# Four graph layers on one core: row sums folded by DMA to the heads' own partitions, gates transposed on VectorE, layer 3 in four column tiles, and tiling changes counted in the plan

## The chip, the cores and the metric

The kernel runs on one core of a Trainium2 chip. A core has TensorE (PE, the matrix engine), VectorE (DVE), ScalarE (ACT), GpSimd (POOL), SyncE (SP, which only issues transfers) and 16 DMA engines. DMAs are issued here from SP's and POOL's queues; those that add to what stands at their destination are issued from POOL. The time is device microseconds of one execution. The median of several runs counts.

## What is computed

32 graphs of 512 nodes with 256 features go through four layers. All share one adjacency matrix. Each layer's output is added to its input and normalised. Cut to what matters:

```python
# x: (32, 512, 256), adj: (512, 512)
def layer0(x):                    # 8 heads of 32
    q, k, v = split(x @ w_qkv)
    attn = softmax(where(adj > 0, q @ k.T / sqrt(32), -1e9))
    x = layernorm(x + attn @ v)
    return layernorm(x + relu(x @ w1 + b1) @ w2 + b2)
def layer1(x):                    # one head, scores s1[n] + s2[m]
    h = x @ W
    return softmax(mask(leaky_relu(s1[:, None] + s2[None, :]))) @ h
def layer2(x):                    # scores (x W1)(x W2)^T
    return relu(softmax(mask(leaky_relu((x @ W1) @ (x @ W2).T))) @ (x @ W3))
def layer3(x):                    # 4 heads of 64, scores as in layer 1
    return elu(softmax(mask(leaky_relu(e_src + e_dst))) @ q)
for layer in (layer0, layer1, layer2, layer3):
    x = layernorm(x + layer(x))
```

## The kernel before

Everything stays in SBUF in float32. A graph's nodes lie in four chunks of 128 partitions (NC = 4), its features in two (KC = 2). Probabilities are kept transposed: a buffer `p` of 128 x 4 x 512 (1 MiB) holds, for 128 source nodes m on the partitions, four stretches of 512 target nodes n. They aren't normalised before they meet the values; the output is divided by the row sums afterwards. In layers 1 and 2 the values carry a column of ones, so that the sums come out of the same matmul. In layers 0 and 3 the outputs are computed transposed (head features on the partitions, nodes along the free axis), and the sums over m are made apart.

PE works in four tilings: full 128 x 128 matmuls; row tiles of 32 x 128 for the scores of layer 0 (`exps`, L1034, four heads side by side); column tiles of 128 x 32 for the outputs of layer 0 (L1093, four heads) and for the sums (L1065, L1281); column tiles of 128 x 64 for the outputs of layer 3 (L1306, two heads). In the plan these are `tiling=0`, 1, 2 and 3.

The row sums of layer 0: for each half of the heads (g) there are four buffers p (m = 0 to 3). `collect` adds them by accumulating DMAs (`add_dma`, issued at L972 on POOL): p1 to p0, p3 to p2, p2 to p0. What is left are two totals, `low` and `high`, with 128 partial sums per head and node. A fold adds the upper 64 partitions of `low` to its lower 64, another the lower 64 of `high` to its upper 64, a copy on SP's queue (L1112) brings these to the upper 64 of `low`, and four matmuls with a constant `pick` (L1065) sum over the partitions. ACT copies the sums out of PSUM (`sums_back`), four transposes (L985) bring nodes onto partitions, and DVE takes reciprocals (L994). Layer 3 has two pairs of buffers; after one add and one fold inside each buffer, four matmuls (L1281) sum. The last graph (`at_once`) sums all buffers on PE instead.

`gates` (layers 1 and 3) needs a row of gate values on all partitions: exponentials into `gs`, one transpose on PE (L1182), a copy by ACT (L1184), a store to DRAM on SP (L1186) and a load that spreads the row over all partitions (L1192, into G). DVE then makes p from G (L1211, L1290).

The order of the work on every engine is made when the program is built. Each piece is recorded as an `Op` with its engine, a cost in ns, its buffers and its tiling. `Plan.place` simulates the engines by these costs: at each step it takes the piece that can start first, and among those the one with the earliest due time. Up to six graphs (WAYS) are under way at once. Due times come from a pace per graph (PACE) and a curve of eleven points, with own curves for the first four and last five graphs. A DMA is two pieces, its issue on POOL or SP and the transfer on one modelled DMA server. The costs only choose the order. On the chip, each engine takes its instructions in that order and waits for its inputs. In `place` before, a change of tiling puts 100 ns (SWITCH) ahead of the piece.

Of the kernel before, what the change touches and what calls it, by code (L numbers as in the profile page):

```python
# [30 lines left out]
PACE = 81.87  # L31
STAY = 0.00
START = (0, 10.17, 59.24, 97.18, 85.64)
EARLY = 186.52

TENTHS = (0, 35.72, 65.32, 68.92, 152.58, 202.32, 246.27, 266.73, 356.34, 362.66, 490.49)
FIRST = (
    (0, 35.72, 65.32, 62.35, 138.44, 202.98, 246.27, 266.73, 356.34, 362.66, 490.49),
    (-28.44, 35.72, 73.98, 55.02, 197, 202.32, 246.27, 266.73, 356.34, 362.66, 490.49),
    (-31.13, 30.72, 65.32, 68.92, 152.58, 202.32, 246.27, 266.73, 356.34, 362.66, 490.49),  # L40
    (0, 35.77, 65.37, 68.97, 152.63, 202.32, 246.27, 266.73, 356.34, 362.66, 490.49),)
LAST = (
    (0, 35.72, 65.32, 68.92, 152.58, 202.32, 246.27, 266.73, 354.73, 363.36, 490.49),
    (0, 35.72, 65.32, 68.92, 152.58, 202.32, 246.27, 266.73, 356.34, 362.66, 490.49),
    (0, 35.72, 65.32, 68.92, 152.58, 202.26, 246.21, 266.73, 356.34, 412.91, 557.81),
    (-0.21, 35.51, 65.11, 68.71, 152.37, 202.11, 226.96, 232.14, 316.44, 341.17, 500.04),
    (-6.23, 29.49, 59.09, 8.93, 61.49, 76.67, 155.18, 191.54, 257.43, 316.36, 394.47),)
# [391 lines left out]
SIGNAL = 70  # L439
SWITCH = 100  # L440
# [11 lines left out]
class Op:  # L452
    def __init__(self, engine, ns, run, graph, rank, port, lag, tiling):
        self.engine, self.ns, self.run, self.graph, self.rank = engine, ns, run, graph, rank
        self.port, self.lag, self.tiling = port, lag, tiling
        self.then, self.missing, self.slots, self.ready = [], 0, [], 0.0


class Plan:
# [19 lines left out]
    def __call__(self, engine, ns, run, reads=(), writes=(), port=False, lag=0, tiling=0):  # L479
        op = Op(engine, ns, run, self.graph, self.rank, port, lag, tiling)  # L480
# [41 lines left out]
    def place(self, urgency, ways, stay=0.0, early=1e12, run=True):  # L522
# [13 lines left out]
        port, port_by, end, tiling = 0.0, None, 0.0, 0  # L536
        self.trace = []
# [21 lines left out]
        while todo:  # L559
            choice = None  # L560
            for e, ops in waiting.items():
                found = []
                for op in ops:
# [8 lines left out]
                    if choice and t > choice[0]:  # L572
                        continue
                    wants = {}
                    for s in op.slots:
                        if s.index is None:
                            wants.setdefault(s.kind, []).append(s)
                    if all(safe(op, kind, new) for kind, new in wants.items()):
                        for kind, new in wants.items():
                            t = max(t, sorted(free[kind])[len(new) - 1][0])  # L580
                        if op.tiling != tiling and e is PE:
                            due += stay
                        found.append((t, due, op))
                if found:
                    best = min(found, key=lambda f: f[:2])
                    if choice is None or best[0] < choice[0]:
                        choice = best
            assert choice, "no instruction can be placed: too few buffers"
            t, _, op = choice
            if op.engine is PE and op.tiling != tiling:  # L590
                t, tiling = max(t, engines[PE] + SWITCH), op.tiling
            waiting[op.engine].remove(op)
# [6 lines left out]
            engines[op.engine] = t + op.ns  # L599
            if op.port:  # L600
                port, port_by = t + op.ns, op.engine
            done = t + op.ns + op.lag + SIGNAL
# [7 lines left out]
            for other in op.then:  # L610
                other.missing -= 1
                other.ready = max(other.ready, done if other.engine != op.engine or op.lag
                                  else t + op.ns)
# [6 lines left out]
            ended[op.graph] = max(ended.get(op.graph, 0.0), t + op.ns + SIGNAL)  # L620
# [9 lines left out]
def fast_path(  # L630
# [50 lines left out]
        "e1": (6, [P, NC * H3]), "gs": (2, [P, NC * H3]), "ri": (3, [P, NC * H0]),  # L681
        "gT": (2, [NC * H3, P]),
# [27 lines left out]
    nc.vector.memset(far, 0.0)  # L710

# [36 lines left out]
    def prepare():  # L748
# [30 lines left out]
        for c in range(NC):  # L779
            dve(690, lambda c=c: nc.vector.tensor_scalar(  # L780
                T(edges)[:, c, :], T(raws[c // 2])[:, c % 2, :].bitcast(I32), 0.0, None, ALU.is_gt),
                [(raws[c // 2], c)], [(edges, c)])
        for m in range(NC):
# [6 lines left out]
            plan(PE, 440, run, [edges], [bank])  # L790
            dve(690, lambda bank=bank, m=m: nc.vector.tensor_copy(T(edge_t)[:, m, :], T(bank)),
                [bank], [(edge_t, m)])
            dve(400, lambda m=m: nc.vector.tensor_scalar(
# [23 lines left out]
        for c in range(NC):  # L817
            off = Slot("e")
            dve(690, lambda c=c, off=off: nc.vector.tensor_tensor(
                T(off), T(edges)[:, c, :], T(raws[c // 2])[:, c % 2, :].bitcast(I32), ALU.not_equal),  # L820
                [edges, (raws[c // 2], c)], [off])
            dve(690, lambda c=c, off=off: nc.vector.tensor_reduce(
# [65 lines left out]
    def evac(dst, to, src, frm, n, writes):  # L888

        act(170 + n * 0.84, lambda: nc.scalar.activation(to(T(dst)), frm(T(src)), AF.Copy),  # L890
            [src], writes)

    def transposed(src, width=0):

        dst = Slot("t")
        for c0 in range(0, NC, 2):
# [7 lines left out]
            plan(PE, 440, run, [(src, c0), (src, c0 + 1)], [bank])  # L904
# [4 lines left out]
    def project_t(w, col, xT, dst, k):  # L909
# [7 lines left out]
        plan(PE, 1720, run, [w, xT], [bank])  # L917
        evac(dst, lambda t: t[:, k, :], bank, lambda b: b, N, [(dst, k)])

    def project(xT, w, col, width, dst):  # L920

        per = N // width
        for c0 in range(0, NC, per):
# [9 lines left out]
            plan(PE, per * KC * width * 1.69, run, [w, xT], [bank])  # L933
# [4 lines left out]
    def normalise(y, dst):  # L938

        st, mv, rs, nm = Slot("st"), Slot("mv"), Slot("rs"), Slot("rs")  # L940
        for c in range(NC):
# [3 lines left out]
            dve(600, run, [(y, c)], [(st, c), (mv, c)])  # L945
# [3 lines left out]
        act(420, deviations, [mv], [rs])  # L949
        dve(300, lambda: nc.vector.scalar_tensor_tensor(  # L950
# [102 lines left out]
    def layer0(xs, at_once):  # L1053
# [27 lines left out]
        for g in range(KC):  # L1081
            av, ps = Slot("bank"), []
            for m in range(NC):
# [14 lines left out]
                if m % 2:  # L1098
                    collect(g, m, ps)
# [337 lines left out]
```

## Time and profile before

| | |
|---|---|
| Median of 3 runs | 2895.84 us (2895.43 to 2897.85) |
| Span of the profiled execution | 2891.7 us |
| PE busy | 2832.4 us, 98% |
| DVE busy | 2443.2 us, 84% |
| ACT busy | 1885.5 us, 65% |
| POOL busy | 865.9 us, 30% |
| DMA engines, mean from 500 to 2500 us | 73% |
| PE busy, 0 to 100, 100 to 200 and 2800 to 2892 us | 83.3, 91.8 and 66.4 us |
| Mean granted TensorE clock | 0.993 |

Busy time is the time in which at least one instruction of the engine was running. Matmuls overlap each other, so their mean duration is longer than their distance from start to start. In the views, a fp32 matmul stands as two records, one for each pass; a transpose as one. "128*32" is the tile of PE. In a view of waits, "A <- B: 9.7, 6, 2.7" says that A waited for B 9.7 us in total, 6 times, 2.7 us at longest. In a timeline the columns are the start in us, the length in us, engine, line, operation, tiles, shapes, and "x8" for eight records merged.

### The profile page before, as it was taken

Reading aid. Unit: us, or ns where it says so; the run is one execution under the profiler, and the core shown is the slowest. Engines: PE = TensorE matmul, PEld = TensorE weight load, DVE = VectorE, ACT = ScalarE, POOL = GpSimd, SP = SyncE. Lnnn points to the kernel's source line nnn. Section 1 sums busy time; section 2 is a strip of 40 time slices with the busy share of each in tenths; the row PEclk is TensorE's granted clock in tenths of the full one; section 3 lists DMA queues with packets and bytes.
Section 4 is the critical chain, followed back from the end, with each engine's and each line's share of the span. In section 5 each row is a group of like instructions: output and inputs, shape, how many; then the busy total and the mean of one; then the engine's idle time right before and its main releaser. Section 6 shows DMA issues by size and latency. Waiting matters only on the chain.

```text
span 2891.7 us, 39629 instructions
## 1 busy us (share of the span) xinstructions
PE 2832.4 (98%) x14014; PEld 1579.2 (55%) x14014; DVE 2443.2 (84%) x4076; ACT 1885.5 (65%) x4104; POOL 865.9 (30%) x962
## 2 busy tenths in 40 slices
PE   8899999999999999999999999999999999999996
PEld 3355555555555555555555555555555555554562
DVE  5568888888888988888988888988888888888877
ACT  4566667666667666666666666666676666676553
POOL 1233333232333232332232333232333323333312
PEclk9999999999999999999999999999999999999998
DMA  6856777777777777777777777776776777775125
GB/s 168 169 110 142 150 159 164 154 144 160 145 161 153 159 149 158 149 160 157 147 152 150 157 157 155 152 160 144 162 157 150 155 153 146 161 163 115 35 55 132
DMA packets 101149, 424.44 MB, mean 147 GB/s; under 512 B 10256, under 2 KB 46224, under 8 KB 59152
## 3 DMA queue, kind: packets, MB, share of 16 engines
q0 software_dynamic: 49600, 325.08, 57.2%
q1 hardware_dynamic: 51344, 96.75, 11.6%
q8 instruction: 113, 1.85, 0.2%
q14 instruction: 92, 0.75, 0.1%
HBM read 63.38 MB, written 17.10 MB: 28 GB/s over the span
## 4 chain that ended last, share of the span: by engine, by line
PE 92%; DVE 3%; DMA 2%; issue 1%; ACT 1%; POOL 0%; SPq 0%; ACTq 0%; DVEq 0%; POOLq 0%
PE bank L929 15%; PE bank L915 11%; PE bank L1034 9%; PE bank L1093 8%; PE bank L1306 8%; PE bank L1221 7%; PE bank L1244 7%; PE bank L1260 7%; PE bank L902 5%; PE bank L1136 4%; PE bank L1148 4%; PE bank L1017 2%; DMA p<-p 1%; PE bank L1281 1%; PE bank L1065 1%
## 5 line engine op out<-in xcount | busy, mean ns | idle before, releaser
L972 POOL DMA_DIRECT2D p<-p x372 | 322.3, 871 | 1787.8 <-DMA p<-p 568.4
L1086 DVE TENSOR_TENSOR p<-p,edge_t 128x2048 f32<-128x2048 f32 x256 | 618.2, 2424 | 59.7 <-ACT p L1038 59.5
L890 ACT ACTIVATE t<-bank 128x512 f32<-128x512 f32 x640 | 373.5, 596 | 384.2 <-PE bank L915 125.4
L1038 ACT ACTIVATE p<-bank 128x512 f32<-128x512 f32 x1024 | 537.9, 599 | 89.2 <-PE bank L1034 87.6
L943 DVE BATCH_NORM_STATS2 st<-y 128x6 f32<-128x256 f32 x768 | 315.9, 411 | 35.6 <-POOL y L960 26.0
L1290 DVE TENSOR_SCALAR p<-p,e,e 128x512 f32<-128x512 f32 x512 | 331.3, 680 | 1.0 <-DMA p<-row 1.0
L960 POOL TENSOR_TENSOR y<-y,x 128x512 f32<-128x512 f32 x192 | 273.7, 1432 | 158.2 <-ACT y L1265 100.1
L1297 DVE TENSOR_TENSOR p<-p,edge_t 128x2048 f32<-128x2048 f32 x128 | 304.9, 2382 | 2.2
L1034 PE MATMUL bank<-t,t 32*128 32x512 f32 x2048 | 302.6, 644 | 0.0
L953 ACT ACTIVATE x<-y,rs,rs 128x256 f32<-128x256 f32 x512 | 277.6, 596 | 24.6 <-DVE rs L950 24.3
L1093 PE MATMUL bank<-p,v 128*32 128x512 f32 x2048 | 275.2, 609 | 12.5 <-DVE p L1086 9.7
L1306 PE MATMUL bank<-p,v 128*64 128x512 f32 x1024 | 242.8, 605 | 3.6 <-DVE p L1297 3.6
L915 PE MATMUL bank<-t,wqkv 128*128 128x512 f32 x512 | 241.6, 595 | 0.7 <-ACT t L890 0.7
L1221 PE MATMUL bank<-v,p 128*128 128x257 f32 x1024 | 237.8, 381 | 0.7 <-DVE p L1214 0.4
L890 ACT ACTIVATE v<-bank 128x264 f32<-128x264 f32 (+2 forms) x384 | 176.5, 460 | 90.2 <-PE bank L929 88.3
L1260 PE MATMUL bank<-v,p 128*128 128x257 f32 x1024 | 227.4, 380 | 0.0
L1244 PE MATMUL bank<-t,t 128*128 128x512 f32 x512 | 225.1, 592 | 0.0
L1221 PEld LDWEIGHTS bank<-v,p 128*128 128x128 f32 x1024 | 189.5, 190 | 40.3 <-issue 16.3
L1260 PEld LDWEIGHTS bank<-v,p 128*128 128x128 f32 x1024 | 194.2, 190 | 28.6 <-issue 1.3
L1034 PEld LDWEIGHTS bank<-t,t 32*128 32x128 f32 x2048 | 86.0, 184 | 169.5 <-issue 101.5
L944 DVE BATCH_NORM_AGGREGATE mv<-st 128x2 f32<-128x6 f32 x768 | 139.7, 182 | 26.3
L902 PE MATMUL bank<-ident,x 128*128 128x128 f32 x1024 | 148.9, 279 | 11.7 <-DMA x<-in_x_dram 7.7
(121 smaller groups left out, 4148.8 us busy)
## 6 DMA issues: line engine op xcount, KB each, us to landing
p<-p POOLq DMA_DIRECT2D x248, 1024.0 KB, 7.2
p<-p POOLq DMA_DIRECT2D x124, 512.0 KB, 5.7
p<-row SPq DMA_DIRECT2D x32, 1024.0 KB
x<-in_x_dram SPq DMA_DIRECT2D x32, 512.0 KB
out_dram<-x SPq DMA_DIRECT2D x32, 512.0 KB
p<-p SPq DMA_DIRECT2D x31, 512.0 KB
e<-row SPq DMA_DIRECT2D x32, 256.0 KB
t<-in_adj_dram SPq DMA_DIRECT2D x4, 256.0 KB
```

The lines of the kernel that those rows point to most:

```text
L890: act(170 + n * 0.84, lambda: nc.scalar.activation(to(T(dst)), frm(T(src)), AF.Copy), [src], writes)
L915: nc.tensor.matmul(T(bank), T(w)[:, i, col:col + P], T(xT)[:, i, :], start=(i == 0), stop=(i == KC - 1))
L929: nc.tensor.matmul(T(bank)[:, j * width:(j + 1) * width], T(xT)[:, k, (c0 + j) * P:(c0 + j + 1) * P], T(w)[:, k, col:col + width], start=( ...
L1034: nc.tensor.matmul(T(banks[j]), T(kT)[r, g, m * P:(m + 1) * P], T(qT)[r, g, :], start=True, stop=True)
L1038: act(600, lambda j=j: nc.scalar.activation(T(p)[:, j, :], T(banks[j]), AF.Exp, scale=1.0 / math.sqrt(D0)), [banks[j]], [(p, j)])
L1086: dve(2420, lambda p=p, m=m: nc.vector.tensor_tensor(T(p), T(p), T(edge_t)[:, m, :].unsqueeze(1).to_broadcast([P, J, N]), ALU.mult), [p, ( ...
L1093: nc.tensor.matmul(T(av)[j * D0:(j + 1) * D0, :], T(v)[:, m, h * D0:(h + 1) * D0], T(p)[:, j, :], start=(m == 0), stop=(m == NC - 1))
L1221: nc.tensor.matmul(T(bank)[:, :C + 1], T(p)[:, m, c * P:(c + 1) * P], T(v)[:, m, 2:C + 3], start=(m == 0), stop=(m == NC - 1))
L1244: nc.tensor.matmul(T(bank), T(xT)[:, k, m * P:(m + 1) * P], T(qT)[:, k, :], start=(k == 0), stop=(k == KC - 1))
L1260: nc.tensor.matmul(T(bank)[:, :C + 1], T(p)[:, m, c * P:(c + 1) * P], T(v)[:, m, :C + 1], start=(m == 0), stop=(m == NC - 1))
L1290: nc.vector.tensor_scalar(T(p)[:, 2 * m + i, :], T(G)[:, h, :], T(e1)[:, r:r + 1], T(e02)[:, r:r + 1], ALU.mult, ALU.max)
L1306: nc.tensor.matmul(T(av)[i * D3:(i + 1) * D3, :], T(q)[:, m0 + m, 2 * H3 + h * D3:2 * H3 + (h + 1) * D3], T(p)[:, 2 * m + i, :], start=(m0 ...
```

## The change

The sums. The matmuls with `pick` are gone except in the last graph. `collect` adds p1, p2 and p3 to p0 one after the other. `halve` then folds the two totals by DMA until each partition belongs to one head: of the upper and lower 64 partitions, one half of the heads' stretches each; then by odd and even partitions, and so on. Each step is an accumulating DMA inside `low`, a plain copy on SP and another accumulating DMA, over half the bytes of the step before. For layer 0 that is 12 DMAs (three of 512 KB, three of 256 KB, six of 64 KB), for layer 3 six (three of 256 KB, three of 128 KB). `rinv_folded` transposes what is left by four PE transposes straight from the buffer; DVE sums the partial sums out of PSUM and takes the reciprocal.

The gates. `gs` and `gT` become 128 x 32. DVE transposes in blocks of 32 x 32, and four small stores on SP write the row to DRAM.

Layer 3. Each head's 64 columns are two matmuls of 32 columns, with the tiling of layer 0's outputs.

The plan. Costs are new throughout. A change of tiling costs SWITCH (92) and then an entry by the tiling entered (121, 34, 104, and 56 for transposes). Each engine has a TAIL, a time from its end to the result. PE takes, of all its ready pieces, that with the least sum of due time, a term by the pair of tilings (CHANGE) and LATE times the wait that it would bring. Each of a graph's pieces has its own due time (DUE), to which curves for the first four and last five graphs are added.

```diff
-SIGNAL = 70
-SWITCH = 100
+SIGNAL = 40
+SWITCH = 92
+ENTRY = {1: 121, 2: 34}
+TAIL = {PE: 160, DVE: 85, ACT: 120, POOL: 45, SP: 0, DMA: 0}
...
+                    key = t, due
+                    if e is PE:
+                        wait = t - engines[PE]
+                        if op.tiling != tiling:
+                            wait = max(wait, SWITCH) + op.entry
+                        key = due + change[tiling][op.tiling] + late * wait, 0
...
+    for gs in buffers["gs"]:
+        nc.gpsimd.memset(gs, 0.0)
...
-        plan(POOL, 950, run, reads, [dst, started])
-        plan(DMA, 5600 if src else 2650, None, reads + [started], [dst], lag=2500)
...
+    def fold(dst, src, slots, mb, accumulate=True):
+        started = Slot(None)
+        if accumulate:
+            plan(POOL, 600, lambda: nc.gpsimd.dma_start(dst(), src(), accum_op=ALU.add),
+                 slots, [slots[0], started])
+        else:
+            plan(SP, 450, lambda: nc.sync.dma_start(dst(), src()), slots, [slots[0], started])
+        plan(DMA, mb * (5000 if accumulate else 3400), None, slots + [started], [slots[0]],
+             lag=1400 if accumulate else 1800)
+    def halve(low, high, heads):
...
+        size = heads / 8
+        fold(lambda: lower(low), lambda: upper(low), [low], size)
+        fold(lambda: upper(low), lambda: upper(high), [low, high], size, False)
+        fold(lambda: upper(low), lambda: lower(high), [low, high], size)
+        step = 2
+        while heads > 1:
+            heads //= 2
+            size /= 2
+            for at in range(step // 2):
+                def part(odd, which, at=at, step=step, w=heads):
+                    rows = T(low)[at + odd * (step // 2)::step]
+                    return rows[:, which * w:(which + 1) * w, :]
+                small = 2 * size / step
+                fold(lambda f=part: f(0, 0), lambda f=part: f(1, 0), [low], small)
+                fold(lambda f=part: f(1, 0), lambda f=part: f(1, 1), [low], small, False)
+                fold(lambda f=part: f(1, 0), lambda f=part: f(0, 1), [low], small)
+            step *= 2
+    def rinv_folded(total, heads):
+        bank, rinv = Slot("bank"), Slot("ri")
         def run():
+            for c in range(NC):
+                nc.tensor.transpose(T(bank)[:, c * P:(c + 1) * P],
+                                    T(total)[:, 0, c * P:(c + 1) * P], ident)
+        plan(PE, 437, run, [total], [bank], entry=56)
+        n = NC * heads
+        dve(610, lambda: nc.vector.tensor_reduce(
+            T(rinv)[:, :n].rearrange("p (s a b) -> p s b a", a=2, b=heads // 4),
+            T(bank).rearrange("p (s r b a) -> p s b a r", s=2 * NC, a=2, b=heads // 4),
+            mybir.AxisListType.X, ALU.add), [bank], [rinv])
+        dve(390 if heads == H0 else 170, lambda: nc.vector.reciprocal(T(rinv)[:, :n], T(rinv)[:, :n]),
+            [rinv], [rinv])
+        return rinv
...
-                add_dma(ps[m - 1], ps[m])
-                if m == 3:
-                    add_dma(ps[0], ps[2])
+            if not at_once:
+                add_dma(ps[0], ps[m])
+                return
...
-            add_dma(low, None, lambda t: (t[:64], t[64:]))
-            add_dma(high, None, lambda t: (t[64:], t[:64]))
...
-            plan(PE, 870, lambda: sums(2, low, True, True), [low], [sm], tiling=2)
-        rinv = rinv0(sm)
+            halve(*totals, J)
+            rinv = rinv_folded(totals[0], H0)
...
-        plan(PE, 150, lambda: nc.tensor.transpose(T(bank)[:R, :P], T(gs)[:, :R], ident),
-             [gs], [bank])
-        act(270, lambda: nc.scalar.activation(T(gT)[:R, :], T(bank)[:R, :P], AF.Copy),
-            [bank], [gT])
-        plan(SP, 450, lambda: nc.sync.dma_start(T(row)[:R, :], T(gT)[:R, :]), [gT], [row], lag=2000)
+        dve(70, lambda: nc.vector.transpose(T(gT), T(gs)), [gs], [gT])
...
+                for j in range(0, P, 32):
+                    nc.sync.dma_start(T(row)[:R, j:j + 32], T(gT)[j:j + R, :])
+        plan(SP, 600, store, [gT], [row], lag=2000)
...
-                            nc.tensor.matmul(T(av)[i * D3:(i + 1) * D3, :],
-                                             T(q)[:, m0 + m, 2 * H3 + h * D3:2 * H3 + (h + 1) * D3],
-                                             T(p)[:, 2 * m + i, :], start=(m0 + m == 0),
-                                             stop=(m0 + m == NC - 1))
-                plan(PE, 1770, run, [q, p], [av], tiling=3)
+                            for w in range(i * D3, (i + 1) * D3, 32):
+                                nc.tensor.matmul(T(av)[w:w + 32, :],
+                                                 T(q)[:, m0 + m, 2 * H3 + k * P + w:2 * H3 + k * P + w + 32],
+                                                 T(p)[:, 2 * m + i, :], start=(m0 + m == 0),
+                                                 stop=(m0 + m == NC - 1))
+                plan(PE, 1742, run, [q, p], [av], tiling=2)
...
-                    add_dma(total, None)
+                    fold(lambda total=total: T(total)[:, 0:2, :],
+                         lambda total=total: T(total)[:, 2:4, :], [total], 0.5)
...
-            plan(PE, 870, lambda: [sums(h, totals[h // 2], h % 2, True, True) for h in range(H3)],
-                 totals, [sm], tiling=2)
-        t = heads_out(oT, rinv3(sm), H3)
+            halve(*totals, 2)
+            rinv = rinv_folded(totals[0], H3)
+        t = heads_out(oT, rinv, H3)
```

## The prediction

> **What bounds the kernel now.** I read the page first, then the stretches of equal length, the waits of PE, and last the timeline of PE in a few microseconds of the steady part.
>
> ```profile
> PE 2832.4 (98%) x14014; PEld 1579.2 (55%) x14014; DVE 2443.2 (84%) x4076; ACT 1885.5 (65%) x4104; POOL 865.9 (30%) x962
> ...
> PE   8899999999999999999999999999999999999996
> ...
> DMA  6856777777777777777777777776776777775125
> ```
>
> PE is busy 98% of the span, and in the stretches from 500 to 2500 us it is busy 499.2 to 499.4 us of every 500. A busy share need not mean useful work, so the waits come next.
>
> ```profile
> PE bank L1093 <- DVE p L1086: 9.7, 6, 2.7
> PE bank L902 <- DMA x<-in_x_dram: 7.7, 1, 7.7
> PE bank L1306 <- DVE p L1297: 3.6, 2, 2.3
> ...
> PE bank L1281 <- DMA p<-p: 2.4, 1, 2.4
> ...
> PE bank L1065 <- DMA p<-p: 1.1, 1, 1.1
> ```
>
> All waits of PE together are some 35 us, and the stretches put them into the first 200 and the last 200 us. In between PE sets the pace: the 32 matmuls of L1260 start every 87.0 us in the chain that ended last (1054.91, 1141.92, 1228.94). So the change is worth what it takes off PE, less any new wait. Durations of single matmuls (595 to 644 ns) overlap and are no price; the distance from start to start is.
>
> ```profile
> 1034.14 0.66 PE L902 MATMUL bank<-ident,x 128*128 128x128 f32 x4
> 1034.64 1.88 PE L915 MATMUL bank<-t,wqkv 128*128 128x512 f32 x4
> 1036.45 1.06 PE L1093 MATMUL bank<-p,v 128*32 128x512 f32 x8
> 1037.45 3.70 PE L915 MATMUL bank<-t,l2m 128*128 128x512 f32 x8
> 1040.98 1.24 PE L929 MATMUL bank<-l2w,t 128*128 128x256 f32 x5
> ```
>
> ```profile
> 1070.58 1.06 PE L1065 MATMUL bank<-p,pick 128*32 128x512 f32 x8
> 1071.57 1.14 PE L1034 MATMUL bank<-t,t 32*128 32x512 f32 x8
> 1072.64 0.66 PE L985 MATMUL bank<-ident,e 128*128 128x128 f32 x4
> 1073.13 0.60 PE L902 MATMUL bank<-ident,x 128*128 128x128 f32 x4
> 1073.57 1.04 PE L929 MATMUL bank<-l1w,t 128*128 128x258 f32 x4
> ```
>
> One pass of 512 columns takes 0.429 us (16 of L1244 from 1044.44 to 1051.30, no change of tiling in them). Eight rows of a 128*32 group are two passes of four tiles side by side, 0.858. What is above these is the price of a change of tiling. The first L915 group takes 1.81 against 1.716: leaving a tiling costs 0.093. The second takes 3.53 against 3.432, ending without a change: entering full tiles costs 0.10. Transposes entered by a change take 0.49, others 0.44: 0.05 to enter. L1034 takes 1.07 for 0.858 and two ends of a change: 0.12 to enter row tiles. L1093 takes 1.00: 0.03 to 0.05 to enter column tiles. A change thus costs 0.21 into row tiles, 0.13 into column tiles, 0.15 (transposes) or 0.20 into full ones.
>
> **The change on PE.** Taken away in each of 31 graphs: the sums of L1065 and of L1281 (0.858 each) and two transposes at L1182 (0.11, the distance from 1078.84 to the next one at 1078.95): 1.94 us. With the last graph's two transposes, and its sums, which stay but pack a little worse, 59.3 us in all. The four transposes of L985 stay in number. L1306 becomes twice as many matmuls, four side by side instead of two: eight per group in two passes of 0.858 is what four cost before; the rows of L1093 show that four column tiles do run side by side. Counted in the order of the two built programs, changes of tiling fall from 1038 to 735: into row tiles 254 and 254, into column tiles (32 or 64 wide) 391 to 239, into full tiles 393 to 242. 152 x 0.127 is 19.3, and 151 x 0.168 (the mean over transposes and others in that order) is 25.4: 44.7 us. PE loses 104.0 us of work, 3.3 us per graph. The order of everything is new, since costs and due times are; the sum holds as long as nothing else ends later than PE.
>
> **The change elsewhere.** ACT loses two copies of 610 ns (L890 into e) and two of 252 (L1184) per graph: it gains slack. DVE gains two sums out of PSUM that no row shows; bounds are 357 (the reciprocal L994 over the same outputs) and 686 (L822, a sum over as many inputs, the nearest, which I take). It also gains two transposes of 128x32, between 70 (the plan's own cost) and 357; the nearest is 223 (L1046, same size). With the reciprocals, which stay, that is 1.8 us per graph, 56 us in all: 2499 of some 2810, 89%. It stays below PE, but its idle share falls from 16 to 11%. The 13.3 us that PE waited for p from DVE, scaled by 16/11, become 20: +7; bounds 0 and 20.
>
> The row sums cost DMA. These are the rows:
>
> ```profile
> q0 software_dynamic: 49600, 325.08, 57.2%
> q1 hardware_dynamic: 51344, 96.75, 11.6%
> ...
> p<-p POOLq DMA_DIRECT2D x248, 1024.0 KB, 7.2
> p<-p POOLq DMA_DIRECT2D x124, 512.0 KB, 5.7
> ```
>
> Accumulated per graph: 10 MiB before (8 of 1 MiB, 4 of a half); after, three quarters and three quarters of a MiB more, 11.5. At 57.2% of the span for 310 MiB, a MiB takes 5.3 us of all engines: +8.0 us. Plain copies grow from 0.5 to 1.25 MiB, at 3.6 us (q1): +2.7. In the steady part DMA is busy 73% of 87 us, 63.6; that becomes 74 of 84, 88%. So it isn't the bound, but a queue that is often full.
>
> Latency matters more. A line through the two medians gives 4.2 + 3.0 us per MiB from issue to landing: 4.95 for a quarter, 4.6 for an eighth, 4.4 for a sixteenth (an estimate; the shortest fold seen took 4.5, so less than 3 is unlikely). Layer 0 gets nine more links, 3 x 4.95 + 6 x 4.4, and its half MiB folds now follow each other (+5.7): 47 us later. Layer 3 gets 3 x 4.95 + 3 x 4.6: 29 us later. What hides it: six graphs are under way, 500 us of PE work. The first transposes of folded sums stand after 109 us of PE work in the new order, the first sums stood after 76. If that cover were gone once, at the start, it would cost 47 - 33 = 14 us; I take 2, the 1.1 us wait seen there and a little. In the steady part PE waited 3.5 us for 62 ends of such chains; five links per graph become twenty, so 14 us, with bounds 0 and 93 (3 us per graph, about the queueing that one link shows between its shortest 4.5 and the usual 7).
>
> The Trainium skill, "DMA: Bandwidth & Descriptors", speaks against such folds: in "Measured (HBM→SBUF, 128 partitions, SWDGE, issued from GpSimd)" it asks for at least 1 MiB per transfer, and in "Anatomy of one DMA — SWDGE (gpsimd) path" it fits 2.0 us plus size at 436 GB/s. By that fit the added links of layer 0 would take some 21 us, by the rows above 41; a fold of half a MiB would take 3.2, where the row has 5.7.
>
> On POOL, 22 issues instead of 12 per graph at 871 ns (group L972) are +8.7 us: 866 becomes 1136 us, 40%. Behind each link that waits for the one before stand the adds of L960, on which normalisation and then PE's transposes wait. SP gets six copies instead of one and eight small row stores of 0.32 us instead of two; behind them stand the loads of x and of G. DVE waits 27.6 us for G now (p L1211 for e from row); twice that still fits into its idle 11%. The memsets and the new costs in the plan run no instruction of weight.
>
> **The sum.** The profiled span is 2891.7; the median of the runs is 4.1 us above it. 2891.7 - 59.3 - 44.7 + 7 + 2 + 14 = 2810.7, and with 4.1, 2815 us. Without new waits it is 2792; waits at the two ends that shrink could give up to 20 us more.
>
> **Rivals.**
> - *The gain is half given back.* PE waits 1.5 to 3 us per graph at its folded sums, or DVE, at 89%, delivers p late. For it: the plan puts PE on exact prices, so PE no longer runs behind its plan and gives others no time. Against it: no steady wait now. 2792 + 31 x 1.5 to 3: 2840 to 2885.
> - *Slower: POOL's queue.* The links of one graph (8 x 7.2, 5 x 5.7, 6 x 4.95, 3 x 4.6, 6 x 4.4) sum to about 156 us, more than a period of 84, so two graphs' chains must interleave on one in-order queue. POOL already waits 568.4 us for DMA p<-p. If one link per graph stands on PE's path, 4.4 x 31 = 136: 2792 + 136 = 2928. It decides from 3.4 us per graph.
> - *The change doesn't do what it says.* If four tiles of L1397 ran in twice the time, +1.7 x 256 = 440 us; the rows of L1093 exclude that. If a change of tiling cost nothing, 45 us of the gain would go: 2860; the distances above speak against it.
>
> **Chances.** Forecast (2790 to 2840): 0.63. Better than that, by shorter ends: 0.07. Half given back: 0.18. Within 0.2% (5.8 us, about what can be told from no change): 0.03. Slower by the POOL queue: 0.09. So 0.88 faster, 0.03 the same, 0.09 slower. The range of 2785 to 2875 leaves out some 0.04 below and 0.16 above.
>
> **What would show it.** Right: the matmuls of layer 2's output start every 83.8 us; PE's groups between changes have the distances above; waits of PE for DMA p<-p are under 20 us; POOL has 682 issues. Wrong: a PE wait of over 2 us per graph at the transposes of p, DMA near 100%, or idle time of DVE that has vanished.

## The result and the profile after

The changed kernel takes 3250.69 us (median of 4 runs, 3240.67 to 3254.29), the kernel before beside it 2895.64. The ratio is 1.1214, with a 95% interval from 1.1194 to 1.1235: 355 us slower. 2815 was predicted, in a range of 2785 to 2875.

From the page of the changed kernel: busy time by engine, and three of the rows of 40 slices.

```profile
PE 2853.2 (88%) x14478; PEld 1630.6 (50%) x14478; DVE 2383.8 (74%) x4202; ACT 1835.0 (57%) x3978; POOL 1203.6 (37%) x1274
...
PE   7868989989889988898988998998899999989994
...
PEclk8889999999999999999999999999999999999997
DMA  6975687777787777877777877777887877785253
```

No engine is full any more. PE is at 88%, DVE fell from 84% to 74%, and the DMA engines stand at seven to eight tenths as before. The clock row hides much (a nine is anything from 0.9), but it begins with eights, and the mean granted clock fell from 0.993 to 0.947. The loss is there all along, as one stretch of equal length shows (its length, then busy time and instructions of PE, weight loads, DVE, ACT and POOL, clock, DMA share and GB/s):

```profile
1000.00:1500.00 500.00, 451.28 (x2275) 260.69 (x2273) 377.74 (x665) 293.08 (x635) 195.61 (x202) 0.96 0.78 161
```

The same stretch of the kernel before:

```profile
1000.00:1500.00 500.00, 499.23 (x2474) 280.00 (x2473) 441.93 (x719) 334.47 (x727) 150.42 (x169) 1.00 0.73 153
```

The matmuls of layer 2's output (L1351, L1260 before) give the period: from 500 to 2600 us the groups start every 97.9 us in the changed kernel (22 groups), every 87.3 before (24 groups). 83.8 was predicted.

What PE waited for in the changed kernel (total us, times, longest):

```profile
PE bank L1312 <- DVE p L1305: 93.8, 24, 7.8
PE bank L1188 <- DVE p L1181: 75.2, 43, 4.4
PE bank L1063 <- DMA p<-p: 72.4, 19, 14.7
PE bank L1063 <- issue: 21.9, 5, 6.4
PE bank L1397 <- DVE p L1388: 21.4, 4, 16.4
PE bank L948 <- ACT x L999: 19.6, 18, 3.3
```

These are many small waits, not one large one: for p from DVE in layers 1, 0 and 3 (190 us), and for the folds at the transposes L1063. DVE in turn waited for others, as its own waits say:

```profile
DVE p L1181 <- ACT p L1135: 180.2, 73, 12.1
DVE st L989 <- POOL y L1006: 153.4, 63, 7.2
DVE ri L1067 <- PE bank L1063: 147.8, 33, 20.7
DVE p L1381 <- DMA p<-row: 96.8, 26, 7.8
```

Before, the last of these was small:

```profile
DVE p L1290 <- DMA p<-row: 1.0, 2, 0.6
```

Each engine waits for another: a late add holds POOL, POOL the normalisation, that DVE or ACT, these PE, and PE ACT again. One such chain, from the chain that ended last (start, length, what; "issue" is time without a visible cause):

```profile
1504.80 7.15 PE bank L1351 x32
...
1525.60 7.38 DMA p<-p
1532.98 0.29 issue
1533.27 0.84 POOL p L1023
...
1534.93 11.22 DMA p<-p
1546.15 0.29 issue
1546.43 10.29 DMA p<-p
1556.72 0.53 DVE p L1381
1557.25 0.47 DVE p L1302
1557.74 2.30 DVE p L1305
1560.18 9.58 PE bank L1312 x32
```

The three transfers here, 7.4, 11.2 and 10.3 us long, are adds of whole buffers (POOL issues them at L1015, at 1525.60, 1534.93 and 1546.43 us). The last is issued when the one before has landed, as the fold at 1533.27 (L1023) is; then DVE can make p, and PE, which has nothing else to do next in its order, starts L1312 7.24 us late. Before, the chain that ended last was 92% PE and 2% DMA. Now:

```profile
PE 45%; DMA 25%; DVE 16%; issue 6%; ACT 4%; POOL 2%; SPq 1%; DVEq 0%; POOLq 0%; ACTq 0%
DMA p<-p 16%; PE bank L975 7%; DMA p<-row 6%; PE bank L1312 5%; PE bank L1397 5%; PE bank L1335 5%; PE bank L1351 4%; PE bank L961 4%; PE bank L1131 3%; PE bank L1188 3%; DVE p L1181 3%; DVE p L1381 2%; PE bank L1237 2%; PE bank L1225 2%; DMA row<-gT 2%
```

The same chain shows a second loss. L1351 and L1312 are 32 matmuls of the same shape. After work without a gap they take 7.15 us, after the gap of 7.24 us 9.58. The granted clock (the third number from the end) is 0.50 in the first 4 us of the slow group and 1.00 in its last 4; two of these stretches:

```profile
1562.00:1564.00 2.00, 2.00 (x6) 1.61 (x5) 1.82 (x2) 2.00 (x5) 1.71 (x1) 0.50 1.00 205
1566.00:1568.00 2.00, 2.00 (x11) 1.76 (x10) 1.57 (x5) 0.00 (x0) 2.00 (x3) 1.00 0.96 197
```

The balance of the spans, in us:

| | span | PE busy | PE idle |
|---|---|---|---|
| before | 2891.7 | 2832.4 | 59.3 |
| predicted work (less 59.3 and 44.7) | | 2728.4 | |
| changed | 3238.9 | 2853.2 | 385.7 |

The idle time grew by 326 us. PE's work, which should have shrunk by 104, takes 125 more than that. 326 + 125 - 104 is the 347 us between the spans. The 125 is counted from the prediction's terms. Against e9 below, which runs as many PE instructions (14478) with 120 us of idle time in place of 386, it is 108 (2853.2 - 2744.9): so much of it comes with the gaps, after which the matmuls run slower.

### The profile page after: what moved, and what is told of

Its sections match the earlier page's. It is cut to its first block, busy times and chain, and to the rows that moved or that the text cites. A ratio compares the mean times of both kernels' runs of the same rounds, so it can differ in the third digit from the quotient of the medians.

```text
span 3238.9 us, 41615 instructions
## 1 busy us (share of the span) xinstructions
PE 2853.2 (88%) x14478; PEld 1630.6 (50%) x14478; DVE 2383.8 (74%) x4202; ACT 1835.0 (57%) x3978; POOL 1203.6 (37%) x1274
## 4 chain that ended last, share of the span: by engine, by line
PE 45%; DMA 25%; DVE 16%; issue 6%; ACT 4%; POOL 2%; SPq 1%; DVEq 0%; POOLq 0%; ACTq 0%
DMA p<-p 16%; PE bank L975 7%; DMA p<-row 6%; PE bank L1312 5%; PE bank L1397 5%; PE bank L1335 5%; PE bank L1351 4%; PE bank L961 4%; PE bank L1131 3%; PE bank L1188 3%; DVE p L1181 3%; DVE p L1381 2%; PE bank L1237 2%; PE bank L1225 2%; DMA row<-gT 2%
## 5 line engine op out<-in xcount | busy, mean ns | idle before, releaser
L1023 POOL DMA_DIRECT2D p<-p x434 | 401.7, 996 | 965.7 <-DMA p<-p 886.9
L1015 POOL DMA_DIRECT2D p<-p x248 | 238.9, 969 | 770.9 <-DMA p<-p 254.5
L1312 PE MATMUL bank<-v,p 128*128 128x257 f32 x1024 | 264.3, 421 | 96.7 <-DVE p L1305 93.8
L1381 DVE TENSOR_SCALAR p<-p,e,e 128x512 f32<-128x512 f32 x512 | 267.9, 565 | 108.9 <-DMA p<-row 96.8
L1188 PE MATMUL bank<-p,v 128*32 128x512 f32 x2048 | 273.1, 623 | 75.3 <-DVE p L1181 75.2
L1006 POOL TENSOR_TENSOR y<-y,x 128x512 f32<-128x512 f32 x192 | 294.0, 1594 | 114.9 <-ACT y L1428 43.4
L1312 PEld LDWEIGHTS bank<-v,p 128*128 128x128 f32 x1024 | 214.9, 213 | 157.6 <-issue 120.1
L936 ACT ACTIVATE v<-bank 128x512 f32<-128x512 f32 (+2 forms) x384 | 175.8, 461 | 203.1 <-PE bank L975 201.9
L1397 PE MATMUL bank<-p,v 128*32 128x512 f32 x2048 | 241.5, 604 | 21.6 <-DVE p L1388 21.4
L1351 PE MATMUL bank<-v,p 128*128 128x257 f32 x1024 | 231.3, 383 | 0.6 <-ACT p L1344 0.6
L1351 PEld LDWEIGHTS bank<-v,p 128*128 128x128 f32 x1024 | 191.5, 190 | 50.1 <-issue 22.9
L999 ACT ACTIVATE y<-y,rs,rs 128x256 f32<-128x256 f32 x256 | 138.1, 592 | 95.2 <-DVE rs L996 89.3
```

The source lines that it names most:

```text
L936: act(55 + n * 0.83, lambda: nc.scalar.activation(to(T(dst)), frm(T(src)), AF.Copy), [src], writes)
L999: act(492, lambda c=c: nc.scalar.activation(T(dst)[:, c, :], T(y)[:, c, :], AF.Identity, bias=T(nm)[:, c:c + 1], scale=T(rs)[:, c:c + 1]), ...
L1023: plan(POOL, 600, lambda: nc.gpsimd.dma_start(dst(), src(), accum_op=ALU.add), slots, [slots[0], started])
L1188: nc.tensor.matmul(T(av)[j * D0:(j + 1) * D0, :], T(v)[:, m, h * D0:(h + 1) * D0], T(p)[:, j, :], start=(m == 0), stop=(m == NC - 1))
L1312: nc.tensor.matmul(T(bank)[:, :C + 1], T(p)[:, m, c * P:(c + 1) * P], T(v)[:, m, 2:C + 3], start=(m == 0), stop=(m == NC - 1))
L1351: nc.tensor.matmul(T(bank)[:, :C + 1], T(p)[:, m, c * P:(c + 1) * P], T(v)[:, m, :C + 1], start=(m == 0), stop=(m == NC - 1))
```

## Experiments

Each line number below is that of the kernel it stands beside; edits shift them by a few. The records and costs in the plan stay those of the kernel that an experiment starts from, so the order on every engine is the same, and only the instructions named are left out, added or replaced. "us" without more are medians; the ratio is to the kernel before on the same chip.

**Is PE the bound, in the old order and in the new?** Three kernels change PE's work by about 3.5 us per graph: one full-tile matmul more in each step of layer 0's q and k (two passes of 0.429 us, four times per graph), or the second half of the contraction left out in two products (L914 for `l2m`, L928 for `l3w`). The outputs of the last are those of half-width products.

```diff
 (e6, e7: after's and before's order)
+            if w is wqkv:
+                nc.tensor.matmul(T(bank), T(w)[:, 0, col:col + P], T(xT)[:, 0, :], start=True, stop=True)
 (e5: before's order)
-            for i in range(KC):
+            n = 1 if w is l2m else KC
+            for i in range(n):
```

> The kernel before in its own order with the same 3.4 us of PE work per graph more, as a control: PE is its bound, so 2897 + 110 = 3007 us, between 2995 and 3015. Less than 2980 would say that PE is not its only bound.

Measured: 3005.19 us, ratio 1.0357 [1.0327, 1.0387]: by the ratio 104 us more, of 110 added. In the old order PE is the bound, as the prediction read it, and its price of a pass is right.

> The changed kernel in its own order, with 3.4 us of PE work per graph more: each of the four L961 groups of layer 0 does its first pass pair twice (4 x 0.858), the result is the same. 32 x 3.43 = 110 us. Theory SLACK (PE waits for late DMAs, so added PE work fills waits, and shorter waits cost less clock): under 3290 us, 0 to 40 above the changed kernel's 3247. Rival ORDER (PE's order is itself the bound): 3340 to 3370.

Measured: 3235.06 us, ratio 1.1149 [1.1071, 1.1227]. 110 us more work for PE cost nothing. PE's time isn't what bounds the new order. The mean clock rose from 0.947 to 0.964: the added matmuls fill part of the gaps.

> The kernel before in its own order, with 3.5 us of PE work per graph less: the second half of the contraction is left out at L915 of layer 2 (two groups, 2 x 0.858) and at L929 of layer 3 (four, 4 x 0.446), so its result is another. 32 x 3.5 = 112 us. Theory SLACK (in the old order every engine but PE is early, because PE's changes of tiling were underpriced and the DMAs overpriced, so a faster PE meets no wait): 2785 to 2815 us, PE waits under 70 us. Rival RESOURCE (some engine or the DMA can't run a graph in 84 us in any order): above 2830.

Measured: 2845.71 us, ratio 0.9807 [0.9779, 0.9836]. Of some 110 us of work taken away (3.5 per graph) only 56 came back as time. PE now waits a little for ACT and DVE in every graph (490 of 500 us busy), and DVE reaches 89%. That is above the 2815 of SLACK and on RESOURCE's side of its line, though it doesn't show RESOURCE: e9 below runs a graph in 84.8 us, which clears the engines, though not the DMA engines, which have few bytes to move there. So even the old order turns only half of what is taken off PE into time.

**What of the change costs it?** Parts are taken out of the changed kernel. Where folds or adds are missing, the row sums of layers 0 and 3 are incomplete and the reciprocals are replaced by a constant, by an instruction of the same size on DVE.

```diff
 (e1: none of the 18 folds per graph issued)
-            plan(POOL, 600, lambda: nc.gpsimd.dma_start(dst(), src(), accum_op=ALU.add),
+            plan(POOL, 600, None,
...
-            plan(SP, 450, lambda: nc.sync.dma_start(dst(), src()), slots, [slots[0], started])
+            plan(SP, 450, None, slots, [slots[0], started])
 (e2: all folds issued, 32 values per partition)
-            return T(t)[64:, 0:w, :]
+            return T(t)[64:, 0:1, 0:32]
```

> The changed kernel in its own order, without the 18 DMAs per graph of `halve` (12 in layer 0, 6 in layer 3); the reciprocal of the folded sums is replaced by a constant of the same size, so the row sums are left out of the result. Theory LINKS (the folds' DMAs, one behind the other in POOL's in-order queue, land later than the order expects, and every engine's fixed order hands that on): PE sets the pace again, 2790 to 2850 us, PE waits under 60 us, clock above 0.98. Rival ORDER (the new order is bad by itself): over 3000. Rival GATES (row stores and loads of G on SP are what is late, folds or not): over 3050.

Measured: 2992.81 us, ratio 1.0325 [1.0304, 1.0345]. The folds are 258 us of the loss, yet without them the kernel is still slower than before and 200 us above the 2792 of a kernel without waits. None of the three theories had it right: the folds are the largest part but not the whole.

> The changed kernel in its own order, all 18 folds per graph issued, but each over 128 bytes per partition in place of 2 to 8 KB (the row sums are left incomplete, a constant stands for their reciprocal). Theory LINKS, by latency: most of the loss stays, above 3050 us. Rival BYTES (the 2.25 MiB more per graph fill the DMA engines and hold up everything behind them): 2790 to 2880 us, near the run without folds.

Measured: 3080.47 us, ratio 1.0627 [1.0606, 1.0648]. That is LINKS by its line, but of the 258 us of the folds the larger part goes with the bytes: issuing the folds and waiting for them costs 88 us, and their bytes 170 more.

```diff
 (e3: one store of 32 columns for a gates row in place of four)
-                for j in range(0, P, 32):
+                for j in range(0, 32, 32):
```

In e3 three quarters of a gates row keep a constant.

> The changed kernel in its own order, with one store of the gates' row on SP in place of four (three quarters of the row are left out and stay at a constant). Theory LINKS: within 60 us of the changed kernel's 3247. Rival GATES: at least 150 us below it, under 3100.

Measured: 3203.95 us, ratio 1.1053 [1.1031, 1.1075]: 47 us less, within LINKS' 60. The prediction had these stores on SP's queue at no cost.

e8 leaves out both, the folds and three of four stores.

> The changed kernel in its own order without the 18 folds per graph, and with one store of the gates' row in place of four (the row sums and three quarters of the gates' row are left out). If the late gates are what is left beside the folds (2993 without folds, and 45 us for the stores alone): 2900 to 2950 us. If what is left is spread over all DMAs and engines, 2960 to 2990.

Measured: 2926.84 us, ratio 1.0087 [1.0057, 1.0116], as expected. e9 leaves out the adds of whole buffers and layer 3's fold inside each buffer (512 KB) too, so that no row is summed in layers 0 and 3.

```diff
 (e9, besides the edits of e8)
-         plan(POOL, 600, lambda: nc.gpsimd.dma_start(T(dst), T(src), accum_op=ALU.add),
+         plan(POOL, 600, None,
```

> Leaves out all row sums of layers 0 and 3 (no adding DMA, no copy between folds; the reciprocals are a constant) and stores each gates row by one DMA. The order of every engine is that of the changed kernel. LATE ADDS: what was left of the loss in e8 (some 135 us over 2792) comes from the adds that stayed there (six links of 1 MiB and two of a quarter per graph, through POOL's queue); then the time falls to 2795-2845. ORDER: the new order makes PE wait for p from VectorE whatever the transfers do, since each engine is filled to its plan; then the time stays at 2880 or above, with waits of PE for p from VectorE of 60 us or more.

Measured: 2865.67 us, ratio 0.9882 [0.9864, 0.9900], between the two theories. A stretch of it:

```profile
1000.00:1500.00 500.00, 497.90 (x2655) 289.88 (x2657) 431.76 (x765) 338.51 (x739) 145.39 (x108) 1.00 0.09 29
```

With no adds on the DMA engines PE is busy 497.9 of 500 us and the period is 84.8 us, one more than predicted. That is the predicted gain in the steady part: the work taken off PE is real. Of the 74 us above 2792, 16 are PE work above the terms (2744.9 us busy for 2728.4). The rest lies mostly at the ends (in the first 200 us PE is busy 154 us, before it was 175), and no add or fold is left to cause it.

**Does the load on the DMA engines delay things in any order?** e10 adds bytes to the kernel before.

```diff
 (e10: before, in one burst)
-            plan(SP, 450, lambda: nc.sync.dma_start(T(low)[64:], T(high)[64:]), totals, [low, started])
+            def copies():
+                nc.sync.dma_start(T(low)[64:], T(high)[64:])
+                for i in range(5):
+                    nc.sync.dma_start(spill[i], T(high)[64:].rearrange("p a b -> p (a b)"))
+            plan(SP, 450, copies, totals, [low, started])
```

> The kernel before, with five plain copies of 512 KB (from high to a scratch in DRAM) added per graph beside the copy of L1112: 2.5 MiB, by q1's price some 9 us of all DMA engines per graph, about what the change adds (10.7). NO SLACK IN THE NEW ORDER: the old order carries the bytes, since its chains of sums have room: 2897-2930, PE still busy 97% or more. BYTES ALONE: load on the DMA engines makes every add and load late in any order: over 3000, PE waiting for DMA p<-p or for p from VectorE by over 100 us.

Measured: 3254.64 us, ratio 1.1224 [1.1203, 1.1244]. The number is that of the theory of bytes alone, but the waits that it named are not there. A group of the page and a wait of PE in e10:

```profile
L954 ACT ACTIVATE x<-y,rs,rs 128x256 f32<-128x256 f32 x512 | 277.8, 596 | 331.4 <-DMA out_dram<-x 308.4
```

```profile
PE bank L986 <- ACT e L891: 258.6, 29, 11.8
...
PE bank L1066 <- DMA p<-p: 1.2, 1, 1.2
```

PE waits 1.2 us for sums at L1066, 12.0 at L1286 (layer 3's) and 22.5 in all for p from DVE. ACT waits 308 us at L954 because a buffer x is still being stored to the output: that store stands behind the five copies on SP's queue and lands after 15.5 us at the median (6.1 in e13 below, 3.3 in e8). Everything on ACT stands behind L954, and PE behind ACT. One store made late once per graph costs 355 us, in the old order too. The run says nothing yet of load. So the same bytes were spread over SP's queue, behind what a graph needs at that moment, in the old order (e13) and in the new one without folds (e14, the kernel of e8).

```diff
 (e13: before; e14: e8)
+    def load():
+        count[0] += 1
+        if count[0] > 12:
+            nc.sync.dma_start(spill[count[0] % 5], flat(T(edge_t)))
...
-        plan(SP, 450, lambda: nc.sync.dma_start(
-            to(), T(row)[:R, :].rearrange("r q -> (r q)").partition_broadcast(P)),
+        plan(SP, 450, lambda: (nc.sync.dma_start(
+            to(), T(row)[:R, :].rearrange("r q -> (r q)").partition_broadcast(P)), load()),
```

(and one `load()` behind the load of x, two behind the store of the output)

> The kernel before, with five copies of 512 KB per graph from a constant to a scratch in DRAM, none ahead of what the graph needs at that moment: one behind each load of G, one behind the load of x, two behind the store of the output. QUEUE: e10's 355 us came from the burst ahead of the output's store, which ACT waited for; spread, the old order carries the load: 2897-2940, ACT's waits for out_dram under 30 us. LOAD: the bytes delay every add and load in the old order too: over 3000, waits of PE for p (from VectorE or DMA) over 100 us.

Measured: 2906.90 us, ratio 1.0030 [1.0018, 1.0041]: 9 us more. From its page, a stretch and two of its transfers (KB each, median us to landing):

```profile
1000.00:1500.00 500.00, 499.47 (x2479) 279.56 (x2476) 436.53 (x717) 336.99 (x732) 157.39 (x171) 1.00 0.82 182
```

```profile
p<-p POOLq DMA_DIRECT2D x248, 1024.0 KB, 8.2
...
p<-p POOLq DMA_DIRECT2D x124, 512.0 KB, 7.3
```

The DMA engines are busier than in the changed kernel (0.82 against 0.78), the big adds land as late (8.2 us; 8.1 there), the half ones later (7.3; 5.4 there), and PE is busy 499.5 of 500 us. In the old order late adds cost some 9 us at most.

> The kernel of e8 (the changed order, without the folds, one store per gates row), with the same five copies per graph at the same places as in e13. NO SLACK: the new order, filled to its plan, hands the same load on: 100 us or more above e8, over 3025. If the load is harmless here too: within 40 us of e8, 2927-2967; then the folds cost by their waits in POOL's queue and not by their bytes.

Measured: 3018.18 us, ratio 1.0412 [1.0367, 1.0457]: 91 us above e8 for the same load, 7 us short of the line that the theory drew and far from the rival's 40. The DMA engines are less busy than in e13, and PE is busy 14 us less of 500 than in e8. The stretch of e8, then that of e14:

```profile
1000.00:1500.00 500.00, 482.75 (x2543) 279.62 (x2542) 411.40 (x726) 325.86 (x710) 174.82 (x162) 0.99 0.64 138
...
1000.00:1500.00 500.00, 468.36 (x2427) 269.77 (x2426) 404.06 (x708) 309.85 (x667) 159.26 (x146) 0.97 0.67 156
```

The adds land hardly later than in e8 (7.8 us at the median for 7.6; the half ones 6.3 for 6.0). What grew most is DVE's wait for layer 3's G (e8, then e14), and PE's wait for layer 1's p with it, from 32.4 to 76.6 us:

```profile
DVE p L1384 <- DMA p<-row: 21.0, 9, 4.7
...
DVE p L1391 <- DMA p<-row: 64.9, 24, 6.4
```

And the copies, though issued by the same lines of code, don't stand at the same distance from what comes next on SP's queue. A copy behind layer 1's load of G, with layer 3's store and load of the gates' row, in e14 and in e13 (start and length in us):

```profile
1242.18 0.43 SPq L738 DMA_DIRECT2D spill<-edge_t  x1
1246.24 0.32 SPq L1286 DMA_DIRECT2D row<-gT  x1
1252.04 0.32 SPq L1293 DMA_DIRECT2D p<-row  x1
...
1260.30 0.59 SPq L694 DMA_DIRECT2D spill<-edge_t  x1
1270.83 0.32 SPq L1193 DMA_DIRECT2D row<-gT  x1
1273.89 0.32 SPq L1199 DMA_DIRECT2D p<-row  x1
```

At the median of 30 graphs the last copy is issued 4.2 us ahead of layer 3's store in e14, 10.5 us in e13. So the 91 us show that this order passes added copies on, but not whether the load on the DMA engines does it or the copies' place on the queue, as in e10.

**Do the parts pay in the old order?**

```diff
 (e4: before, layer 3 as in the change; e11: with e12's edit too)
-                            nc.tensor.matmul(T(av)[i * D3:(i + 1) * D3, :],
+                            for w in range(i * D3, (i + 1) * D3, 32):
+                                nc.tensor.matmul(T(av)[w:w + 32, :],
 (e12: before, gates' rows as in the change, four stores)
-        plan(PE, 150, lambda: nc.tensor.transpose(T(bank)[:R, :P], T(gs)[:, :R], ident),
-             [gs], [bank])
+        plan(PE, 150, lambda: nc.vector.transpose(T(gT), T(gs)), [gs], [bank, gT])
```

> The kernel before in its own order, with layer 3's output in four column tiles of 32 in place of two of 64, and nothing else. By the prices read from its profile 59 changes between the two widths of column tiles go, 59 x 0.127 = 7.5 us: 2888 us. If four column tiles out of one buffer run slower than two, it is above 2900.

> The kernel before with the gates' part of the change alone, its order kept. If the gates' part is what gains in e11, the time is that of e11 within 6 us (ratio 0.995-0.999); if four stores cost anywhere, over 2910.

> The kernel before with two parts of the change and its own order kept: the gates' rows transposed on VectorE with four stores each, and layer 3 in four column tiles. PE loses two transposes and two changes of tiling or so per graph. BOTH HARMLESS OUTSIDE THE NEW ORDER: 2880-2892, ratio 0.994-0.999, PE busy 97-98%. STORES COST ANYWHERE: four stores make G late here too (e3 gave 45 us for them): over 2910, with waits of PE for p from VectorE of over 40 us.

Measured: 2896.11 us for the tiles (ratio 0.9993 [0.9982, 1.0004]), 2901.82 for the gates (1.0009 [0.9999, 1.0018]), 2893.81 for both (0.9982 [0.9972, 0.9991]). Alone neither shows; together they give 5 us by the ratio and the fastest of the kernels that leave nothing out. PE's busy time falls by 14 us in it, more than the time. What was expected of both is met in the ratio (the time is 2 us above its range), what was expected of each alone isn't. Four stores cost at most 5 us here and 47 in the new order; but here a PE transpose and a copy by ACT ahead of the stores are gone, so the pair is not quite alike.

The same edit in the two orders, in us:

| edit | old order | new order |
|---|---|---|
| 2.5 MiB more of copies per graph, spread, in the new order nearer to the gates' stores | +9 (e13) | +91 (e14 over e8) |
| four stores of a gates row instead of one | +3, at most 5 by its interval, a PE transpose and an ACT copy per row gone as well (e12) | +47 (changed kernel over e3) |
| some 3.4 us more PE work per graph | +104 (e7) | none (e6) |

## Why the prediction was wrong

**Right: the bound before and PE's work.** e7 shows PE as the bound. Without adds, folds and three of four stores, PE's busy time is 2744.9 us where the terms gave 2728.4, and the period 84.8 where 83.8 was forecast (e9). Four column tiles cost what two did (L1397: 241.5 us busy, L1306 before: 242.8).

**Right: most prices elsewhere.** The sums out of PSUM take 686 ns on DVE as taken, the small transposes 202 for 223, POOL has its 682 issues (but at 969 and 996 ns for 871: 1204 us busy for 1136).

```profile
q0 software_dynamic: 70432, 373.86, 60.6%
q1 hardware_dynamic: 65600, 121.15, 12.8%
...
p<-p POOLq DMA_DIRECT2D x248, 1024.0 KB, 8.1
p<-p POOLq DMA_DIRECT2D x124, 512.0 KB, 5.4
...
p<-p POOLq DMA_DIRECT2D x124, 256.0 KB, 5.1
...
p<-p POOLq DMA_DIRECT2D x124, 64.0 KB, 5.9
p<-p POOLq DMA_DIRECT2D x62, 128.0 KB, 7.1
```

These are the queues and the issues of the changed kernel. In time of all 16 engines q0 grew by 1963 - 1654 = 309 us, 10.0 per graph for 8.0 predicted, q1 by 2.6 for 2.7. The links that POOL issues for one graph take 145 us by these medians; by those of the prediction 127. The new chains are 14% longer than estimated, mostly because the small folds are not faster than the large ones.

**Wrong: "What hides it: six graphs are under way, 500 us of PE work."** This step sized the loss by the waits of the old order (3.5 us for 62 chain ends, made four times as much, 14 us, at most 93), as if the cover were a property of the kernel. In the new order it isn't there: the folds alone cost 258 us (e1), the adds of whole buffers and the folds of 512 KB that e8 still has cost 61, with adds that land after 7.6 us (e8 over e9). In the old order adds that land after 8.2 us cost some 9 us more than those after 7.2 (e13). What the step left out is 97.9 - 83.8 = 14.1 us per graph, 437 us over 31 graphs, which is the error of the prediction (436). Counted from 2792, the sum without any new wait, the loss is 459 us. By single steps, in the order in which they were taken out: the folds' bytes 170, their issue and waiting 88, the stores 66 (47 where the folds are there), the lateness of the adds that were left 61, and 74 that remain without any add (16 of them PE work that the terms were short of). The sizes depend on the order of taking out.

Not all of this is the order's doing. PE has less work now behind which a wait can hide, and e5 shows what that does in the old order: of some 110 us taken off PE 56 come back, so the forecast gain wasn't there in full even with the old chains of sums. On the other hand e6 gives PE about its old amount of work in the new order, and the time stays at 3235 us. No run has the folds in the old order; how much of their 258 us it would have covered stays open.

**Wrong with it: DVE's +7 us and SP's queue at nothing.** DVE's share was taken from 84% to 89% and its lateness scaled by idle share. DVE fell to 74% and made PE wait 190 us where it was 13, not for lack of time but because its inputs were late. An engine's idle share says how much work fits, not when its inputs come. "Twice that still fits into its idle 11%" failed for the same reason: its waits for G are 104 us where they were 29, 96.8 of them for layer 3's (L1381). What the prediction named to show it wrong (waits of over 2 us per graph at the transposes of p) happened, with 72.4 us for p<-p alone.

**The start** was mis-sized in the way the prediction had priced: 14 us if cover is gone, 2 taken. The longest wait at L1063 in the first 200 us is 14.7, and in all PE is busy 31 us less there than before (143.6 for 175.0).

**Left out: the clock.** The loss from waiting was counted as waiting only. The gaps also slowed the work between them, by 108 of the 125 us in PE's balance above.

**The rivals.** "POOL's queue" had the sign, and its first step, POOL waiting for a chain's link:

```profile
POOL p L1023 <- DMA p<-p: 886.9, 218, 11.5
POOL p L1015 <- DMA p<-p: 254.5, 45, 11.0
```

That is 1141 us where it was 568. But it priced one link of 4.4 us per graph on PE's path and so came to 2928; the delay spread to DVE, ACT and the loads of G, and was three times that. "Half given back" gave the reason, PE on exact prices that gives others no time, but at most a fifth of the size. That PE's new prices are what took the cover away is argued, not shown: a new order with the old prices, or with longer transfers in its plan, wasn't tried. e5 shows half the gain given back in the old order with the old prices.

## What to carry to other kernels

When a change makes a new static order, the waits of the old one need not tell what the new one hides; what should be asked of it is how late each input may come. A pair of runs with the same added load in both orders (here 9 against 91 us) tests that, if the load also stands equally far ahead of what is needed next in both. A chain of small dependent transfers costs more than its bytes' share of the engines: with almost no bytes the folds still cost 88 us here, with them 258. So it is to be priced per link, with its bytes, and with what stands behind it on the queue. And a gap on TensorE is to be priced above its length, since the matmuls behind it run slower (here 108 us of it to 326 us of new idle time).

## What was not expected of the hardware

The granted clock. Single gaps were enough: 32 matmuls took 9.58 us after a gap of 7.24 us, 7.15 without, with a clock of 0.50 in the first 4 us. The mean clocks of the runs fall with PE's idle time: 0.993 (before, 59 us idle), 0.987 (e9, 120), 0.983 (e8, 162), 0.947 (changed, 386). The Trainium skill, "TensorE: Matmul & The Clock Gate", section "HAM oscillation — how this bites in real kernels", warns of idle gaps above some 3.4 us, after which matmuls run at half rate; the trace here agrees for this gap of 7.24 us (no run here shows where the limit lies), and the 108 us above show that it is no small term.

Small accumulating transfers. Folds of 128 and 64 KB landed after 7.1 and 5.9 us, those of 256 and 512 KB after 5.1 and 5.4; with 8 and 4 KB (e2) it was 3.7 and 5.1. The smallest of each run (64 and 4 KB) take every fourth partition; those of 128 KB take every second, but so do half of those of 256. Whether that is the cause, or their place in the queue, was not tried.
